# Who adds lam for the third row block, and where feed-forward's normalization reads and runs

## The chip, the cores and the metric

The kernel runs on one core of a Trainium2 chip. A core has a matrix engine (PE, with its weight loads shown as PEld), a vector engine (DVE), a scalar engine for activation functions (ACT), a general engine (POOL, called gpsimd in the code) and a queue engine that issues transfers (SP). Each runs its own queue of instructions in order; they meet through semaphores. Matmuls write to PSUM banks; DVE and ACT read both PSUM and SBUF, and POOL's instructions in this kernel read SBUF alone. The metric is the device time of one execution in microseconds (us).

## The reference

The input is `x` of 8 sequences, 512 tokens, 128 channels, all fp32. Two parts follow each other, each added to its input.

The first part normalizes `x` over channels, projects to 16 heads of 8 channels, and weighs causally, not with a softmax but with weights `1/(lam - s)`, where `lam`, one number for each query, is found by four Newton rounds:

```
lam = s_masked.max(-1) + 1.0
for _ in range(4):
    d = maximum(lam - s, EPS);  w = where(mask, 1/d, 0)
    f = w.sum(-1) - 1.0;        fp = -where(mask, 1/d**2, 0).sum(-1)
    lam = lam - f / fp
p = where(mask, 1/maximum(lam - s, EPS), 0);  p = p / p.sum(-1);  out = p @ V
```

The second part normalizes again and runs six layers. A layer is windowed attention (16 heads of 64 channels, windows of 32 keys with the window before, queries and keys normalized and rotated) and then feed-forward: shift half of the channels by one token, normalize over channels, scale and add, two matmuls to 341 columns each, gelu of one times the other, a matmul back to 128 columns.

## The kernel before

**Two parts woven together.** The first part of sequences 0 and 1 runs alone at the start, as two streams step by step. From about 600 us on the second part runs, sequence by sequence and layer by layer, and the first part of the other six sequences is fed in between. A unit is one layer of one sequence (48 of them); a unit takes eight slots, one for each pair of heads. A slot is one turn of the `while` loop, and `tick(n)` at twelve places in it lets the first part go on by a planned number of steps, so that the first part is used up at slot 232 of 384. After that the second part runs alone. Units go in groups: layers 0 to 5 of sequences 0 and 1 in turn (units 0 to 11), then sequences 2, 3 and 4, then 5, 6 and 7.

**A Newton round.** Four heads of a sequence make a batch; a batch has four rounds, and there are 32 batches, so 128 rounds. The scores lie negated in `ns`, one tile for each row block `rb` of 128 queries, in four pieces `a` of different width: a query sees only the keys up to its own 32-query piece, so block 3 has pieces of 416, 448, 480 and 512 columns, block 2 of 288, 320, 352 and 384, block 1 of 160 to 256, block 0 of 32 to 128. `lam` differs from piece to piece. A round needs `Ln(ns + lam)`, then `Exp(-that)`, which is the weight, then sums of the weights and of their squares, which DVE takes with one statistics instruction for each piece (L289). Seven short DVE instructions (`step`, L336 to L345) turn these into the new `lam`.

For blocks 3 and 2, `evaluations` lets ACT add `lam` itself, as the bias of the Ln; since the bias differs for each piece, that is one Ln for each piece (L301, four for a block). The Exp needs no bias and takes two pieces at once, a half of a block (L309). For blocks 1 and 0, `add_lam` (L276) has POOL add `lam` piece by piece into a tile `df`, and ACT takes the whole block with one Ln (L316) and one Exp (L321). In `newton`, POOL's adds are issued ahead of the ACT work of the round. After the fourth round of a batch the same `add_lam` adds the final `lam` to all four blocks (into `ns`, 16 instructions), and `attend_weigh` (L349, L351) takes Ln and Exp of these; this is issued in the first round of the next batch.

**Feed-forward.** `feed_forward` is a generator whose parts, between its `yield`s, are issued one by one by `further()`. While units of sequences 0 and 1 are under way (`dense`), there are four such places in each slot, otherwise one. The parts are: shift (POOL, L635 to L637); transpose into a PSUM bank `px` (PE, L833), copy it to SBUF as `xt` (ACT, L835), statistics from `xt` (DVE, L839 and L840); reciprocal deviation `rn` by Ln and Exp (ACT, L843 and L844) and the normalization of `xt` in four instructions (POOL, L846); transpose back (PE, L853) and scale and add (ACT, L855); the gate matmuls; gelu and the other matmuls; the last matmul and the sum.

**What sets the order.** The code's order gives priorities. The tile framework has a planner that fixes each engine's queue ahead of the run, by its own estimate of when an instruction's inputs are there, so a later instruction can stand ahead of an earlier one; `follow` is used where an order must hold. On the chip the queues then run in that order. PSUM banks for all of this come from one pool of five (`ps_a`, through `bank`). The tile `d` of a Newton round has two buffers of block 3's width; `df1` and `df0` have one each.

Of the kernel before, what the change touches and what calls it, by code (L numbers as in the profile page):

```python
# [9 lines left out]
F32 = mybir.dt.float32  # L10
BF16 = mybir.dt.bfloat16
AF = mybir.ActivationFunctionType
# [4 lines left out]
P = 128  # L17
# [33 lines left out]
def tile_kernel(  # L51
# [18 lines left out]
    nc = tc.nc  # L70
# [96 lines left out]
    def streams(pools, bank1):  # L167
# [70 lines left out]
        def width(rb):  # L238
            return sum(keys(rb, a) for a in range(4))
# [53 lines left out]
        def evaluations(t):  # L293

            late = []
            for rb in (3, 2):
                d = dp.tile([P, width(3)], F32, name="d")[:, 0 : width(rb)]
                for h in range(2):
                    for a in (2 * h, 2 * h + 1):
                        c = 4 * rb + a  # L300
                        nc.scalar.activation(  # L301
                            pieces(d, rb)[a], pieces(t["ns"][rb], rb)[a], AF.Ln,
                            bias=t["lam"][:, c : c + 1],
                        )
                    if late:
                        statistics(t, *late.pop(0))
                    yield
                    e = halves(d, rb)[h]
                    nc.scalar.activation(e, e, AF.Exp, scale=-1.0)  # L309
                    if late:  # L310
                        statistics(t, *late.pop(0))
                    yield
                    late += [(d, rb, 2 * h), (d, rb, 2 * h + 1)]
            for rb in (1, 0):
                d = t["df"][rb]
                nc.scalar.activation(d, d, AF.Ln)  # L316
                if late:
                    statistics(t, *late.pop(0))
                if rb:
                    yield  # L320
                nc.scalar.activation(d, d, AF.Exp, scale=-1.0)  # L321
                if late:
                    statistics(t, *late.pop(0))
                yield
                late += [(d, rb, a) for a in range(4)]
            for n in (3, 3, 2):
                for _ in range(n):
                    if late:
                        statistics(t, *late.pop(0))
                yield  # L330
# [87 lines left out]
        def stieltjes(seqs):  # L418
# [36 lines left out]
            def newton(now, k):  # L455
                if k == 0:
                    first_lam(now)
                    yield
                now["st"] = sm.tile([P, H, 2, 3], F32, name="stw")
                now["df"] = {}  # L460
                for rb in (1, 0):
                    now["df"][rb] = d = dp.tile([P, width(rb)], F32, name=f"df{rb}", bufs=1)
                    add_lam(now, d, rb)
                yield
                yield from evaluations(now)
                step(now)
                yield
# [359 lines left out]
    def feed_forward(u, w1, w2):  # L827
# [3 lines left out]
        px = bank([P, NT, D], "px")  # L831
        for c in range(NT):
            nc.tensor.transpose(px[:, c, :], xs[:, c * P : (c + 1) * P], ident)  # L833
        xt = tp.tile([P, NT, D], F32, name="xt", tag="ff")
        nc.scalar.copy(xt, px)  # L835
        st = tp.tile([P, NT, 6], F32, name="st")
        mv = tp.tile([P, NT, 2], F32, name="mv")
        for c in range(NT):
            nc.vector.bn_stats(st[:, c, :], xt[:, c, :])  # L839
            nc.vector.bn_aggr(mv[:, c, :], st[:, c, :])  # L840
        yield
        rn = tp.tile([P, NT], F32, name="rn")
        nc.scalar.activation(rn, mv[:, :, 1], AF.Ln, bias=eps_ln)  # L843
        nc.scalar.activation(rn, rn, AF.Exp, scale=-0.5)  # L844
        for c in range(NT):
            nc.gpsimd.tensor_scalar(  # L846
                xt[:, c, :], xt[:, c, :], mv[:, c, 0:1], rn[:, c : c + 1],
                ALU.subtract, ALU.mult,
            )
        yield  # L850
# [241 lines left out]
```

## Time and profile before

| | us |
|---|---|
| median of three runs | 4686.6 (4683.49 to 4689.29) |
| profiled execution | 4683.56 |
| its span, first to last instruction | 4681.8 |
| busy: PE, DVE, ACT, POOL | 4029.8, 3935.3, 3532.1, 3177.3 |
| L301, Ln with lam as bias, 1024 instructions | 590.4 |
| L309, Exp of blocks 3 and 2, 512 | 441.2 |
| L276, POOL's adds in the rounds, 1024 | 400.3 |
| L846, POOL's normalization in feed-forward, 192 | 150.2 |

How to read the lines below. A group line names the line of code, the engine, the operation, out<-in, shapes and the count, then the busy time and the mean of one instruction in ns, then the idle time of the engine just before it and what ended it. A line of waits says who waited for whom: us in total, times, the longest. The chain of waits is followed back from the last instruction, at each step to what released it; a piece shows its start, its length and who did it. A table by stretches of the span gives for each stretch its length, then each engine's busy time (and number of instructions), the granted clock, the share of the transfer engines and GB/s. `x4` at the end of a line means four instructions. Instructions that follow at once on ACT and DVE overlap by about a tenth of a microsecond, so that what one costs in a busy stretch is read from start to start.

### The profile page before, as it was taken

How to read it: one execution, taken by the hardware profiler on the slowest of the kernel's cores; microseconds unless marked ns; L12 is line 12 of the kernel's file. 1: busy time of each engine (PE TensorE's matmuls, PEld its weight loads, DVE VectorE, ACT ScalarE, POOL GpSimd, SP SyncE). 2: the span in 40 equal slices, each digit the busy share in tenths (PEclk: the TensorE clock that was granted, in tenths of full speed). 3: DMA queues.
4: the chain of work that ended last, by engine and by line, in shares of the span. 5: the costliest groups of instructions: out<-in, count | busy, mean ns of one | idle time of the engine just before them, and what ended most of it. 6: DMA issues, size and time to landing. Idle time of an engine off the chain costs nothing.

```text
span 4681.8 us, 165984 instructions
## 1 busy us (share of the span) xinstructions
PE 4029.8 (86%) x68749; PEld 2507.4 (54%) x68749; DVE 3935.3 (84%) x8788; ACT 3532.1 (75%) x6716; POOL 3177.3 (68%) x4081
## 2 busy tenths in 40 slices
PE   4344688887888888898988999998999999999998
PEld 1233455554455544555555555555666666666665
DVE  7878788887888888998998999999787788877785
ACT  7998677777788777888887888888666666666664
POOL 4543666666666666776777767777787777777774
PEclk7667799999999999999999999999999999999999
DMA  1000222222122222232222222222243333333332
GB/s 49 1 1 1 67 59 51 62 55 59 46 66 61 60 53 62 62 72 50 59 67 54 69 54 70 53 59 68 66 102 83 85 90 75 88 79 86 89 75 59
DMA packets 558912, 288.87 MB, mean 62 GB/s; under 512 B 97580, under 2 KB 541264, under 8 KB 558160
## 3 DMA queue, kind: packets, MB, share of 16 engines
q1 hardware_dynamic: 558160, 278.26, 25.4%
q8 instruction: 543, 8.90, 0.8%
q14 instruction: 209, 1.71, 0.1%
HBM read 66.21 MB, written 7.34 MB: 16 GB/s over the span
## 4 chain that ended last, share of the span: by engine, by line
PE 41%; ACT 26%; DVE 22%; POOL 8%; issue 2%; DMA 1%; SPq 1%; ACTq 0%; POOLq 0%; DVEq 0%
PE m L667 8%; ACT d L301 7%; ACT d L309 5%; PE ptq L733 4%; PE pv L704 4%; DVE stw L289 4%; PE acc L812 4%; DVE qr L672 4%; PE po L787 3%; PE s L752 3%; PE pT L776 3%; POOL ns L276 3%; DVE raw L689 3%; ACT sq L678 2%; PE s L263 2%
## 5 line engine op out<-in xcount | busy, mean ns | idle before, releaser
L682 POOL TENSOR_TENSOR qn<-qr 128x512 f32<-128x512 f32 x768 | 970.0, 1280 | 493.6 <-DVE qr L672 440.5
L672 DVE TENSOR_TENSOR qr<-m,tab 128x1024 f32<-128x1024 f32 x768 | 913.5, 1217 | 157.7 <-PE m L667 116.2
L695 POOL TENSOR_TENSOR qn<-qn,ss 128x512 f32<-128x512 f32 x768 | 786.3, 1046 | 299.5 <-ACT ss L692 285.2
L667 PE MATMUL m<-wqkv,xs 128*128 128x512 f32 x1536 | 759.4, 608 | 16.1 <-ACT prT L777 3.7
L678 ACT ACTIVATE sq<-m 128x512 f32<-128x512 f32 x768 | 459.5, 600 | 394.1 <-DVE qr L672 385.1
L301 ACT ACTIVATE d<-ns,lam 128x416 f32<-128x416 f32 (+7 forms) x1024 | 590.4, 625 | 91.6 <-DVE lam L345 71.0
L289 DVE BATCH_NORM_STATS2 stw<-d 128x6 f32<-128x480 f32 (+7 forms) x1024 | 545.8, 563 | 122.7 <-ACT d L309 120.3
L276 POOL TENSOR_TENSOR df<-ns,lam 128x160 f32<-128x160 f32 (+7 forms) x1024 | 400.3, 429 | 307.2 <-DVE sw L343 135.6
L763 POOL TENSOR_TENSOR pr<-pr,nm 128x512 f32<-128x512 f32 x384 | 401.2, 1045 | 253.2 <-DVE ss L690 146.2
L738 ACT COPY qT<-ptq 128x512 f32<-128x512 f32 x768 | 425.0, 586 | 184.5 <-PE ptq L733 183.4
L689 DVE TENSOR_REDUCE raw<-sq 128x16 f32<-128x1024 f32 x384 | 466.6, 1215 | 64.5 <-ACT sq L678 53.2
L733 PEld LDWEIGHTS ptq<-ident,qn 128*128 128x128 f32 x3072 | 364.7, 144 | 207.9 <-issue 110.4
L733 PE MATMUL ptq<-ident,qn 128*128 128x128 f32 x3072 | 428.2, 281 | 34.3 <-POOL qn L695 20.3
L812 PE MATMUL acc<-oT,wo 128*128 128x512 f32 x768 | 414.6, 622 | 39.0 <-ACT oT L808 38.1
L704 PE MATMUL pv<-wqkv,xs 128*128 128x256 f32 x1536 | 440.3, 410 | 7.7 <-ACT sq L678 5.8
L309 ACT ACTIVATE d<-d 128x864 f32<-128x864 f32 (+3 forms) x512 | 441.2, 871 | 0.0
L364 PE MATMUL dTp<-ident,ns 128*128 128x128 f32 x1280 | 231.3, 302 | 184.1 <-POOL ns L276 119.1
L667 PEld LDWEIGHTS m<-wqkv,xs 128*128 128x128 f32 x1536 | 259.8, 194 | 206.6 <-issue 136.6
L787 PE MATMUL po<-v,prT 64*32 64x65 f32 x24576 | 348.5, 226 | 20.3 <-DVE pr L757 19.7
L752 PE MATMUL s<-qT,qT 64*32 64x64 f32 x24576 | 355.8, 226 | 6.0 <-ACT qT L738 5.0
L787 PEld LDWEIGHTS po<-v,prT 64*32 64x32 f32 x24576 | 278.5, 106 | 129.8 <-issue 52.8
L263 PE MATMUL s<-kn,qj 32*32 32x288 f32 (+14 forms) x4096 | 321.2, 419 | 23.0 <-DVE mn L267 17.6
(137 smaller groups left out, 7984.3 us busy)
## 6 DMA issues: line engine op xcount, KB each, us to landing
v<-v SPq DMA_DIRECT2D x2304, 65.0 KB
v<-v SPq DMA_DIRECT2D x768, 48.8 KB
wqkv<-in_L_ffn_Wqkv_dram SPq DMA_DIRECT2D x72, 256.0 KB
v<-v SPq DMA_DIRECT2D x384, 32.5 KB
wqkv<-in_L_ffn_Wqkv_dram SPq DMA_DIRECT2D x72, 128.0 KB
wo<-in_L_ffn_Wo_dram SPq DMA_DIRECT2D x36, 256.0 KB
tab<-tabs SPq DMA_DIRECT2D x36, 256.0 KB
w<-in_L_ffn_W_dram SPq DMA_DIRECT2D x18, 341.0 KB
```

The costliest lines, as they stand in the source:

```text
L289: nc.vector.bn_stats(t["st"][:, 4 * rb + a].rearrange("p u k -> p (u k)"), pieces(d, rb)[a])
L301: nc.scalar.activation(pieces(d, rb)[a], pieces(t["ns"][rb], rb)[a], AF.Ln, bias=t["lam"][:, c : c + 1],)
L309: nc.scalar.activation(e, e, AF.Exp, scale=-1.0)
L667: nc.tensor.matmul(m.rearrange("p t h e -> p t (h e)"), lhsT=xs[:, c * P : (c + 1) * P], rhs=wqkv[:, 0:2, q0 : q0 + HQ * DHL], start=True, ...
L672: nc.vector.tensor_tensor(qr, m.unsqueeze(1).to_broadcast([P, 2, 2, HQ, DHL]), tab[:, i].rearrange("p (k t) e -> p k t e", k=2).unsqueeze( ...
L682: nc.gpsimd.tensor_tensor(g["qn"][:, c].rearrange("p t h (u e) -> p (t h) u e", u=2), halves_of[:, 0], halves_of[:, 1, :, ::-1, :], ALU.add,)
L689: nc.vector.tensor_reduce(raw[:, :, :, 0], sq, axis=AX.X, op=ALU.add)
L695: nc.gpsimd.tensor_tensor(qc, qc, ss[:, i, :].unsqueeze(2).to_broadcast([P, 2 * HQ, DHL]), ALU.mult)
L704: nc.tensor.matmul(pv[:, i], lhsT=xs[:, c * P : (c + 1) * P], rhs=cols, start=True, stop=True,)
L733: nc.tensor.transpose(pt[:, c * P : (c + 1) * P], g["qn"][:, c, t, 2 * p : 2 * p + 2, :].rearrange("p h e -> p (h e)"), ident,)
L787: nc.tensor.matmul(po[u * QB : (u + 1) * QB, e, c, :], lhsT=prT[rows, c, u * QB : (u + 1) * QB], rhs=g["v3"][rows, n, p, :], start=True, s ...
L812: nc.tensor.matmul(acc, lhsT=wo[:, pp % (NPAIR // 2), :], rhs=a["oT"], start=(pp == 0), stop=(pp == NPAIR - 1),)
```

## The change

In `evaluations`, block 2 goes the way of blocks 1 and 0: POOL adds `lam` to its four pieces, into a tile `df2` (first of the three blocks in `newton`), and ACT takes Ln of a half at a time, without bias, in place in `df2`. Block 3 stays as it was; its tile `d3` has one buffer, so that both blocks together need less room than the two buffers of `d` did.

In `feed_forward`, as long as the first part is not used up (`near`), the copy to `xt` is gone: the statistics read the transposed block in its PSUM bank, and DVE, not POOL, normalizes from the bank into `xt`. One `yield` is gone too, so that transpose, statistics, `rn` and normalization are issued as one part. After the first part has ended, feed-forward is as before.

```diff
@@ evaluations
             for rb in (3, 2):
-                d = dp.tile([P, width(3)], F32, name="d")[:, 0 : width(rb)]
+                d = dp.tile([P, width(3)], F32, name="d3", bufs=1) if rb == 3 else t["df"][2]
                 for h in range(2):
-                    for a in (2 * h, 2 * h + 1):
-                        c = 4 * rb + a
-                        nc.scalar.activation(
-                            pieces(d, rb)[a], pieces(t["ns"][rb], rb)[a], AF.Ln,
-                            bias=t["lam"][:, c : c + 1],
-                        )
+                    e = halves(d, rb)[h]
+                    if rb == 3:
+                        for a in (2 * h, 2 * h + 1):
+                            c = 4 * rb + a
+                            nc.scalar.activation(
+                                pieces(d, rb)[a], pieces(t["ns"][rb], rb)[a], AF.Ln,
+                                bias=t["lam"][:, c : c + 1],
+                            )
+                    else:
+                        nc.scalar.activation(e, e, AF.Ln)
...
@@ newton
-                for rb in (1, 0):
+                for rb in (2, 1, 0):
                     now["df"][rb] = d = dp.tile([P, width(rb)], F32, name=f"df{rb}", bufs=1)
                     add_lam(now, d, rb)
@@ feed_forward
+        near = done_steps < total
         xt = tp.tile([P, NT, D], F32, name="xt", tag="ff")
-        nc.scalar.copy(xt, px)
+        if not near:
+            nc.scalar.copy(xt, px)
+        src = px if near else xt
         st = tp.tile([P, NT, 6], F32, name="st")
         mv = tp.tile([P, NT, 2], F32, name="mv")
         for c in range(NT):
-            nc.vector.bn_stats(st[:, c, :], xt[:, c, :])
+            nc.vector.bn_stats(st[:, c, :], src[:, c, :])
             nc.vector.bn_aggr(mv[:, c, :], st[:, c, :])
-        yield
+        if not near:
+            yield
         rn = tp.tile([P, NT], F32, name="rn")
...
         for c in range(NT):
-            nc.gpsimd.tensor_scalar(
-                xt[:, c, :], xt[:, c, :], mv[:, c, 0:1], rn[:, c : c + 1],
+            (nc.vector if near else nc.gpsimd).tensor_scalar(
+                xt[:, c, :], src[:, c, :], mv[:, c, 0:1], rn[:, c : c + 1],
                 ALU.subtract, ALU.mult,
             )
```

More of the change, by code (lines that the diff above doesn't have):

```diff
@@ L307, in evaluations @@
                     yield
-                    e = halves(d, rb)[h]
                     nc.scalar.activation(e, e, AF.Exp, scale=-1.0)
```

## The prediction

> **What bounds the kernel now.** I read the busy table by stretches first, cut where the work changes: two streams of the first part (110 to 520 us), the woven stretch with units 0 to 10 (600 to 1880), the woven rest (1880 to 3260), the second part alone.
>
> ```profile
> core 0: us, PE busy (x) PEld busy (x) DVE busy (x) ACT busy (x) POOL busy (x), PEclk, DMA share, GB/s
> 110.00:520.00 410.00, 186.00 (x1837) 116.05 (x1837) 323.43 (x1101) 368.82 (x607) 191.72 (x409) 0.66 0.04 12
> 600.00:1880.00 1280.00, 1078.60 (x17486) 646.57 (x17486) 1088.95 (x2571) 998.52 (x1875) 837.28 (x1121) 0.94 0.24 57
> 1880.00:3260.00 1380.00, 1258.67 (x21566) 759.97 (x21559) 1259.78 (x2881) 1136.18 (x2172) 996.94 (x1291) 0.98 0.27 62
> 3260.00:4682.00 1422.00, 1393.94 (x26288) 925.54 (x26287) 1105.76 (x1740) 892.65 (x1817) 1043.42 (x1054) 0.99 0.35 81
> ```
>
> ACT is 90% busy in the first stretch; in the woven ones nobody is full (PE and DVE 84 to 91%, ACT 78 and 82%, POOL 65 and 72%); the last is PE's, and the change leaves it alone. So I next added up the chain of waits in each stretch: 110 to 520 is ACT 58%, DVE 22%, POOL 8%; 600 to 1880 is ACT 30%, DVE 27%, PE 25%, POOL 13%; 1880 to 3260 is ACT 36%, DVE 34%, PE 18%, POOL 8%. Before 110 ACT has 34%. These shares are my price of a microsecond: one on ACT after 1880 is worth 0.36.
>
> Pieces of that chain in the first stretch, two streams in step, give the costs of block 2:
>
> ```profile
> 204.54 1.76 ACT d L301 x4
> 206.30 1.20 ACT d L309 x2
> 207.50 1.97 ACT d L301 x4
> 209.46 1.41 ACT d L309 x2
> ```
>
> The reader is to see that two Lns with bias (288 and 320 columns) take 0.88 for a stream, the one Exp over the same 608 columns 0.60; for 352 and 384 it is 0.985 against 0.705.
>
> In the woven stretch with units 0 to 10, feed-forward stops everybody. Counting slots by their two copies L738, the two slots with feed-forward's middle take 19.3 us each, the others about 11.6. The chain there, then the timeline of the same place, then the waits of the stretch:
>
> ```profile
> 1000.80 3.12 POOL xt L846 x4
> 1003.92 0.04 issue
> 1003.97 0.48 PE pn L853
> 1004.44 1.71 PE ptq L733 x8
> ```
>
> ```profile
> 1004.48 0.78 ACT L855 ACTIVATE xn_ffn<-pn,vec 128x512 f32<-128x512 f32 x1 [4.28 <-PE pn L853]
> 1008.17 2.36 DVE L672 TENSOR_TENSOR qr<-m,tab 128x1024 f32<-128x1024 f32 x2 [8.37 <-PE m L667]
> ```
>
> ```profile
> PE pn L853 <- POOL xt L846: 53.3, 44, 9.7
> ACT xn_ffn L855 <- PE pn L853: 44.0, 11, 9.0
> ```
>
> PE stands before the transposes until POOL has normalized, ACT and DVE stand behind PE. All 44 normalizations of these 11 units are on the chain, 34.3 us.
>
> **Part 1, block 2 on ACT.** A round loses two Lns' starts and the bias reads: 0.88 + 0.985 - 0.60 - 0.705 = 0.56 us, in 128 rounds 72 us of ACT. By chain shares: 7 rounds before 110 (x 0.56 x 0.34 = 1.3), 30 to 520 (x 0.58 = 9.7), 43 to 1880 (x 0.30 = 7.2), 45 after (x 0.36 = 9.1). Gain 11.0 alone, 16.3 woven; 72 at the very most, nothing at least, if `lam` still comes from DVE when it does now.
>
> **Part 1, block 2 on POOL.** The same adds exist after each batch:
>
> ```profile
> L276 POOL TENSOR_TENSOR ns<-ns,lam 128x384 f32<-128x384 f32 x32 | 26.6, 831 | 0.0
> L276 POOL TENSOR_TENSOR ns<-ns,lam 128x352 f32<-128x352 f32 x32 | 24.9, 777 | 0.0
> L276 POOL TENSOR_TENSOR ns<-ns,lam 128x320 f32<-128x320 f32 x32 | 23.1, 723 | 0.0
> L276 POOL TENSOR_TENSOR ns<-ns,lam 128x288 f32<-128x288 f32 x32 | 21.4, 669 | 0.1
> ```
>
> A round pays 3.00 us, ahead of the 3.4 of blocks 1 and 0; 128 make 384 us, POOL's share rises from 0.65 to 0.73 and from 0.72 to 0.79 in the woven stretches (feed-forward's normalization taken off).
>
> Is ACT kept waiting? It takes block 3 first. From the start of POOL's first add to ACT's first Ln of block 2 there are 5.7 us (median) in the first woven stretch, 4.7 in the second, and the two pieces it wants take 1.39. Put in front of the present adds, they would be late three times in 128, 7 us together: I take nothing for it. The cover is block 3's four Lns and two Exps.
>
> What is queued behind on POOL pays: `qn` (L682, L695; PE's transposes and the two `qr` buffers wait for these), `pr` (L763; ACT's Exp), the adds for `attend_weigh`. I pushed POOL's queue back by 3 us after each round's adds, less the idle time met on the way, and compared each end with its consumer's start. Feed-forward's own part left out, some consumer would be late in 6 of 43 rounds of the first woven stretch and in 11 of 45 after; the worst lateness of each such round sums to 21 and 44 us. That is the ceiling, 65, if each moves the end. By chain share it is 3.0 x 43 x 0.105 (POOL's 13% without L846) = 13.5 and 3.0 x 45 x 0.08 = 10.8: 24. A queue that meets idle time forgives, so I take 24, floor zero.
>
> Alone, POOL has room (47% busy) except in the first round of a batch, where the 6 us of both streams go ahead of 19 us of `attend_weigh` adds: compared likewise, ACT would wait 1.7, 1.7, 3.0 and 6.0 more, 12 in all; the planner can put other ACT work first, and I take 4.
>
> DVE pays too. Its short instructions with two operands in SBUF last longer when POOL is at work:
>
> ```profile
> L338 DVE TENSOR_TENSOR stw<-s,stw x128: 156/204/1283, 48.6 to 3269.9; 128x32 f32<-128x32 f32 x128
> L345 DVE SCALAR_TENSOR_TENSOR lam<-sw,lam x128: 150/174/972, 55.8 to 3273.9; 128x16 f32<-128x16 f32 x128
> ```
>
> (minimum, median and maximum ns.) L336, L338, L342, L344 and L345 together lie 0.83 us a round over what they take beside an idle POOL. A tenth more POOL is 0.083 x 88 rounds x 0.3 = 2. The Trainium skill's page SBUF — State Buffer, section SBUF: two separate sides, speaks against the change here: DVE and GpSimd share a port pair that whoever starts first holds for a whole instruction, and a DVE instruction with two SBUF inputs is blocked until then. By that rule each of the five would wait half of a 0.75 us add with 0.07 more probability, which is 0.13 x 88 = 12 us of DVE, an estimate, twice the trace's 7 before shares. The trace's own maxima (1283 against 156) agree with blocking; the sum keeps 2.
>
> `d3` with one buffer costs nothing: the next round's first Ln needs `lam`, and `lam` needs all statistics of this one.
>
> **Part 2, feed-forward, units 0 to 10.** POOL's four at 798 ns go (34.3), DVE's four come. No row shows a per-partition normalization from PSUM of 128 columns; L382, a 128-column copy from PSUM, has 278 ns, L864, scalar addition from PSUM, 740 at 512 columns, which less 384 columns at the 1.04 ns of L289's rows is 339. I take 330, nearest the operation: 14.5 us. Gain 20. POOL also began 19 us later, summed over the 11, than `rn` was done, because it was at `qn`, `pr` or adds; DVE is idle just there (8.37 above), but has its own queue, so half: 9.5. The copy frees 0.60 x 11 of ACT, x 0.30 = 2. Statistics from the bank cost what they did (278 from PSUM against 269). Together 31.5. Floor 10: with the `yield` gone DVE stands at the normalization until ACT has done `rn` (0.52 us plus up to 1.6 of ACT's queue), and behind it stand `qr` and the statistics, on which POOL and ACT wait. Ceiling 60: all 44 us that ACT stands before L855, and what follows being issued a quarter of a slot earlier. The bank `px` is held until the normalization instead of until the copy, some 4 us, one of five; PE is stopped in that time anyway, so nothing.
>
> **Part 2, units 11 to 27.** Here feed-forward waits for nobody (L846 hardly shows in the chain), so there is little to win: DVE +17 x 1.32 x 0.34 = 7.5 lost; DVE standing for `rn`, 1 us each, 6 lost; ACT 17 x 0.60 x 0.36 = 3.7 and POOL 17 x 3.13 x 0.08 = 4.3 won. Net 5.5 lost, between 8 won and 25 lost. No transfer is issued elsewhere, and SP's queue is passed by nothing.
>
> **Sum.** -11 + 4 (alone), -16.3 + 24 + 2 (woven rounds), -31.5 + 5.5 (feed-forward) = -23 us on the profiled 4683.6, which is 3.0 under the median: 4686.6 - 23 = 4664 after rounding, 0.5% faster.
>
> **Rivals.** *POOL's added adds decide (slower).* Place: `qn` and `pr` behind the adds. For it: POOL has 13% of the chain at only 65% busy, and 17 rounds with late consumers. Against it: the other 71 rounds meet idle time soon enough. Without its term the sum is -47, so it decides from 47 of the 65 on; at the ceiling the time is 4686.6 - 47 + 65 = 4705. *The stop at feed-forward only changes its owner.* DVE's queue takes POOL's place and the gain is the floor, 10: about 4686, no change. For it: DVE is 85% busy there. Against: its 8 us of idle at that very place. *The stop goes altogether*, for which speak ACT's 44 us: 60 in place of 31.5, time 4635.
>
> **How the numbers follow.** A measurement of this kernel tells about 0.2% (9 us) from no change. Forecast 0.44, stop gone 0.14, owner changed 0.15, POOL decides 0.27. The forecast alone spans 4640 to 4680 and its upper edge is in the band of no change. Faster 0.57, same 0.14, slower 0.29. The range reaches from "stop gone" with POOL's adds at their floor (4635 - 24 = 4611) to POOL at its ceiling with feed-forward at its floor (4705 + 21.5 = 4726).
>
> **What would show it.** L301 has 512 instructions, L276 in the rounds 1536, POOL's busy time grows by about 384 - 28 x 3.13 = 300, ACT's falls by 72 + 17 = 89, DVE's grows by 37 or more. Right: in the two feed-forward slots of units 0 to 10 PE's wait before L853 falls under 20 us in sum and the slots to about 17.7; up to 520 us the same work ends about 7 us sooner. Wrong: waits of PE, ACT or DVE for L682, L695 and L763 that grow by more than 50 us; ACT before block 2's Ln waiting for POOL; or a new wait of DVE for `rn`. The planner orders all queues anew, which can move the woven stretches either way by an amount no row of before tells.

## The result: 0.4% slower, and the profile after

The changed kernel takes 4706.13 us (median of five executions, 4702.6 to 4708.96) against 4687.67 (4683.49 to 4689.73) for the kernel before, beside which it was run: 18.5 us more, ratio 1.0042 [1.0031, 1.0054]. The forecast was 4664, faster. The profiled execution took 4707.44 us, its span is 4705.7, which is 23.9 over the span before; places are compared below between profiled executions, so that their sums are held against 23.9, not 18.5.

The table by stretches of the kernel after, with the columns of before (length, busy time of PE, PE's weight loads, DVE, ACT and POOL with the number of instructions, granted clock, share of the transfer engines, GB/s):

```profile
core 0: us, PE busy (x) PEld busy (x) DVE busy (x) ACT busy (x) POOL busy (x), PEclk, DMA share, GB/s
110.00:520.00 410.00, 194.35 (x1817) 117.73 (x1818) 325.06 (x1091) 347.19 (x532) 268.70 (x525) 0.62 0.04 11
600.00:1880.00 1280.00, 1085.30 (x17778) 649.38 (x17777) 1121.74 (x2660) 978.20 (x1797) 934.29 (x1267) 0.94 0.25 58
1880.00:3260.00 1380.00, 1244.64 (x21008) 747.71 (x21006) 1247.52 (x2863) 1086.07 (x2024) 1053.87 (x1382) 0.98 0.26 61
3260.00:4700.00 1440.00, 1411.81 (x26718) 937.88 (x26716) 1128.53 (x1796) 908.69 (x1851) 1055.43 (x1070) 0.99 0.35 81
```

What was meant to move has moved. In the first stretch ACT is 22 us less busy and POOL 77 more, in the woven ones ACT 20 and 50 less, POOL 97 and 57 more; 1880 to 3260 also holds less of everybody's work, since the same work now takes longer. The groups of the adds and of the Ln with bias, after:

```profile
L276 POOL TENSOR_TENSOR df<-ns,lam 128x288 f32<-128x288 f32 (+11 forms) x1536 | 761.3, 533 | 218.8 <-DVE lam L348 97.8
L303 ACT ACTIVATE d<-ns,lam 128x416 f32<-128x416 f32 (+3 forms) x512 | 324.2, 677 | 116.4 <-DVE lam L348 101.4
```

The counts are those announced, 1536 and 512 (lines lie two or three further down in the code after, up to seven in feed-forward). ACT's idle time just before these Lns was 91.6 us in the kernel before (L301) and is 116.4 now: ACT has less to do and waits longer for `lam`.

Block 2's Ln costs what was said. Pieces of the chain of waits, after (start, length, who):

```profile
284.91 0.60 ACT df L308
285.51 0.36 ACT ns L354
285.87 0.60 ACT df L308
```

Two pieces (608 columns) take ACT 0.60 us, where two Lns with bias took 0.88.

The stop at feed-forward has gone from units 0 to 10. The waits of 600 to 1880, after:

```profile
PE pn L860 <- DVE xt L853: 8.0, 6, 3.0
ACT xn_ffn L862 <- PE pn L860: 2.2, 2, 2.0
```

These were 53.3 and 44.0. Who holds the chain in the first stretch has changed as well. The shares by line between 110 and 520 us, the first line from before, the second from after:

```profile
by line: ACT d L301 21.2%; ACT d L309 15.5%; DVE stw L289 10.6%; ACT ns L351 5.1%; ACT df L316 5.1%; DVE dT L367 4.9%; ACT ns L349 4.9%; ACT df L321 4.3%; PE po L378 3.7%; POOL ns L276 3.4%; issue 2.8%; PE s L263 2.6%; POOL df L276 2.0%; DV
```

```profile
by line: DVE stw L289 15.7%; POOL df L276 13.7%; POOL ns L276 10.8%; DVE dT L370 8.2%; PE s L263 6.0%; issue 5.3%; PE po L381 4.5%; ACT d L303 3.2%; DVE s L339 3.1%; ACT d L312 3.0%; ACT df L308 2.6%; ACT df L312 2.4%; ACT df L319 2.2%; ACT
```

ACT's 58% have become 17, POOL's 8% have become 27 and DVE's 22% have become 37. ACT was relieved so far that other engines took its place.

**Where the time went.** A slot can be found in every trace by ACT's two copies `qT`. The start of the same slot in two profiled executions, one minus the other, gives the lead or loss up to there. The marks are slot 8 (617 us in before), slot 96 (1831), slot 224 (3309, shortly before the first part is used up). Feed-forward of units 0 to 10 lies between the first two, that of units 11 to 27 nearly all between the last two. The last column ends at the last slot. In us against before:

```
                       to slot 8   8 to 96   96 to 224   after 224
after                     +8.8      -20.5      +35.9       +0.9
forecast                  -7        -24         +8          0
```

(The forecast's parts, put to their stretches: -7.2 + 13.5 + 1 - 31.5 and -9.1 + 10.8 + 1 + 5.5.) The stretch with the stop came out nearly as forecast, but by luck, as the last part shows. The loss is at the start, 16 us off the forecast, and in units 11 to 27, 28 off.

How well such a reading repeats: four kernels below (e2, e3, e5, e6) have the same code in units 0 to 10 and read -22.7, -24.6, -24.9 and -21.7 in the second column. Kernels below that leave units 11 to 27 as they were (e7, e10, e11, and e3 but for unit 11) read +2 to +8 in the third; what is left there is the planner's new order and the state in which they enter. Seven whose code at the start is that of before (e2, e3, e5, e6, e10, e11, e17) read +0.2 to -3.6 in the first. So about 4 us in the first column, 3 in the second and 8 in the third mean nothing. The columns come from one profiled execution of each kernel: their sums differ by up to 7 us from the difference of the medians, and in e10, whose profiled execution is its fastest, by 9.

### The profile page after: what moved, and what is told of

It is laid out like the page before. It is cut to its first block, busy times and chain, and to the rows that moved or that the text cites. A ratio compares the mean times of both kernels' runs of the same rounds, so it can differ in the third digit from the quotient of the medians.

```text
span 4705.7 us, 166329 instructions
## 1 busy us (share of the span) xinstructions
PE 4048.6 (86%) x68749; PEld 2510.4 (53%) x68749; DVE 3984.4 (85%) x8900; ACT 3449.2 (73%) x6430; POOL 3447.3 (73%) x4481
## 4 chain that ended last, share of the span: by engine, by line
PE 40%; ACT 23%; DVE 22%; POOL 10%; issue 3%; DMA 1%; SPq 0%; ACTq 0%; POOLq 0%; DVEq 0%
PE m L670 7%; DVE stw L289 5%; PE pv L707 4%; PE ptq L736 4%; PE acc L815 4%; ACT d L303 4%; PE po L790 3%; POOL ns L276 3%; DVE qr L675 3%; POOL df L276 3%; PE s L755 3%; DVE raw L692 3%; ACT d L312 3%; PE pT L779 2%; ACT sq L681 2%
## 5 line engine op out<-in xcount | busy, mean ns | idle before, releaser
L276 POOL TENSOR_TENSOR df<-ns,lam 128x288 f32<-128x288 f32 (+11 forms) x1536 | 761.3, 533 | 218.8 <-DVE lam L348 97.8
L289 DVE BATCH_NORM_STATS2 stw<-df 128x6 f32<-128x160 f32 (+11 forms) x1536 | 482.5, 360 | 46.4 <-ACT df L324 24.1
L736 PE MATMUL ptq<-ident,qn 128*128 128x128 f32 x3072 | 418.6, 277 | 44.4 <-POOL qn L698 22.9
L303 ACT ACTIVATE d<-ns,lam 128x416 f32<-128x416 f32 (+3 forms) x512 | 324.2, 677 | 116.4 <-DVE lam L348 101.4
L790 PE MATMUL po<-v,prT 64*32 64x65 f32 x24576 | 359.0, 228 | 28.7 <-DVE pr L760 28.3
L289 DVE BATCH_NORM_STATS2 stw<-d 128x6 f32<-128x416 f32 (+3 forms) x512 | 306.6, 630 | 58.2 <-ACT d L312 57.9
```

The costliest lines, as they stand in the source:

```text
L276: nc.gpsimd.tensor_tensor(o, n, by.to_broadcast([P, keys(rb, a)]), ALU.add)
L289: nc.vector.bn_stats(t["st"][:, 4 * rb + a].rearrange("p u k -> p (u k)"), pieces(d, rb)[a])
L736: nc.tensor.transpose(pt[:, c * P : (c + 1) * P], g["qn"][:, c, t, 2 * p : 2 * p + 2, :].rearrange("p h e -> p (h e)"), ident,)
L790: nc.tensor.matmul(po[u * QB : (u + 1) * QB, e, c, :], lhsT=prT[rows, c, u * QB : (u + 1) * QB], rhs=g["v3"][rows, n, p, :], start=True, s ...
```

## Experiments: the two halves of the change alone

Is the loss POOL's added adds, or feed-forward?

e1_block2: the changes to `evaluations` and `newton`, with `feed_forward` as before. Its core:

```diff
-                for rb in (1, 0):
+                for rb in (2, 1, 0):
...
+                    else:
+                        nc.scalar.activation(e, e, AF.Ln)
```

> The first part of the change alone: POOL adds lam for block 2, feed-forward as before. The changed kernel came out 18.5 us slower; by equal slots it lost 9 us before the second part is under way, won 20 in units 0 to 10, lost 36 in units 11 to 27. Theory POOL (the added adds cost it, in the rest above all): about 9 us lost before slot 8, 5 to 15 in units 0 to 10, 25 to 35 in units 11 to 27, near 4730 in all. Theory FEED (DVE's normalization and its stop for rn cost it in units 11 to 27): only the 9 us at the start are lost and the woven stretches win up to 8, near 4690. Theory ORDER (the planner's new order, not any one cost): the effects of this run and the next do not add up to the changed kernel's, by more than 15 us.

e2_ffn: the changes to `feed_forward` alone. Its core:

```diff
+        near = done_steps < total
...
-        yield
+        if not near:
+            yield
...
-            nc.gpsimd.tensor_scalar(
+            (nc.vector if near else nc.gpsimd).tensor_scalar(
```

> The second part alone: feed-forward from its bank while the first part lasts, block 2 on ACT as before. Theory POOL: the start is unchanged, 25 to 35 us are won in units 0 to 10, units 11 to 27 lose no more than 8, near 4660. Theory FEED: about 25 us are won in units 0 to 10, 25 to 35 lost in units 11 to 27, near 4690. Theory ORDER: neither sum holds.

Measured: e1 4750.49 against 4685.91, ratio 1.0141 [1.0125, 1.0156], 64.6 us slower. e2 4691.6, ratio 1.0014 [1.0005, 1.0023], 5.7 slower. By stretches:

```
              to slot 8   8 to 96   96 to 224
e1_block2        +7.2      +26.0      +32.5
e2_ffn           -3.6      -22.7      +30.8
after            +8.8      -20.5      +35.9
```

Neither half is any good alone, and they don't add: 70 apart, 18.5 together. So e1 by itself went roughly as POOL said (with more lost in units 0 to 10), e2 by itself as FEED said, and the sum of the two misses by 52 us, which is ORDER's sign; that the planner's order is the reason is not shown by it. Feed-forward gives 23 of the 31.5 forecast in units 0 to 10 and loses all of it in the rest, where a loss of 5.5 was forecast. Block 2 alone costs 26 and 32, near the ceiling of the rival *POOL's added adds decide* (21 and 44); together with feed-forward's part it costs 2 and 5.

## Experiments: what feed-forward's three edits do

The diff in `feed_forward` holds three things that the prediction had in one sum: statistics from the bank without the copy, normalization on DVE, and one `yield` less. Two theories for the gain in units 0 to 10: the shorter normalization does it (call it NORM), or that what follows is issued a quarter of a slot earlier (EARLIER).

e3_ffn_early, e2 only while units 0 to 11 are under way, and e10 and e11, which part the edits there:

```diff
 # e3: e2, but
-        near = done_steps < total
+        near = len(groups_of) > 1 and b in groups_of[0]
 # e10: before, without the yield in units 0 to 10
-        yield
+        if u > 10:
+            yield
 # e11: bank and DVE in units 0 to 10, the yield kept
+        near = u <= 10
...
-        if not near:
-            yield
+        yield
```

> The second part alone and only for sequences 0 and 1 (units 0 to 11), block 2 on ACT as before. Both theories: 25 to 35 us won in units 0 to 10 and nothing moved before or after, 4653 to 4662. By POOL it differs from the run with all 28 units by less than 8 us, by FEED it is 25 to 35 us faster than that.

> Units 0 to 10 lose only the yield; copy on ACT and normalization on POOL stay, block 2 and the other units as before. All of feed-forward's change there won 24 us from slot 8 to 96. Theory NORM (POOL's 3.1 us and its queue were the stop): 0 to 8 of the 24. Theory EARLIER (issuing the rest a quarter of a slot sooner did it): 14 to 24.

> Units 0 to 10: statistics from the bank and normalization on DVE, but the yield kept between them; everything else as before. Theory NORM: 16 to 24 of the 24 us from slot 8 to 96. Theory EARLIER: 0 to 8.

Measured: e3 4665.77 against 4685.91, 0.9960 [0.9948, 0.9973]; e10 4703.23 against 4682.51, 1.0044 [1.0029, 1.0059]; e11 4640.02, 0.9912 [0.9897, 0.9927]. In units 0 to 10 (slots 8 to 96): e3 -24.6, e10 +8.5, e11 -46.7. Two kernels below with the same code there as e11 read -45.6 (e14) and -50.0 (e17). The whole of e3 came out 26 us under e2, as FEED said.

NORM is right, EARLIER falls: the missing `yield` costs 8.5 alone (by e10's median the loss is larger, 21 us in the whole) and 22 on top of the shorter normalization. Waits of 600 to 1880 in e10, then in e11:

```profile
PE pn L854 <- POOL xt L847: 51.1, 44, 9.5
ACT xn_ffn L856 <- PE pn L854: 44.8, 11, 9.5
```

```profile
ACT xn_ffn L858 <- PE pn L856: 14.4, 9, 6.3
PE pn L856 <- DVE xt L849: 13.0, 9, 3.4
```

The reader is to see that the wait is no measure of the time here: e11 waits 14.4 us before `xn_ffn`, e3 and after only 2.3 and 2.2, and e11 is the faster by 22. What the milestones of a unit say (means in us after the first transpose into `px`, over units 0 to 10):

```
                     normalized   gate matmuls start   gelu starts   last matmul ends
before                  12.3            19.4              26.4            31.8
e10 (yield gone)        12.1            14.3              26.8            32.3
e11 (bank, DVE)          8.7            14.9              22.7            28.4
e3 (both)                7.9            10.9              22.7            28.1
```

Without the `yield` the gate matmuls start 4 to 5 us sooner, and gelu comes no sooner at all. So PE's time for the gate is taken from other work ahead of need; that this is where the 22 us go was not tried apart. The mean length of a slot by its place among eight: the two slots with feed-forward's middle last 20.0 and 19.8 us before, 16.9 and 19.4 in e11, 20.9 and 16.5 in e3; the other six together 70.6, 69.8 and 70.7. Both orders shorten one slot by three; without the `yield` the long slot is 1.5 longer than in e11, the short one 0.4 shorter and the six 0.8 longer.

One thing is not parted from this, the granted clock of PE. Between slots 8 and 96 its mean was 0.937 in before, 0.930 in e10, 0.947 in e3 and 0.961 in e11, in the order of the times, and PE's busy time for the same work was 1021.9, 1020.7, 1010.2 and 1004.9 us. In before the clock was halved 24 times in this stretch, each time behind 3.4 us in which PE had been busy for 55% or less. So a shorter stop of PE can bring the higher clock; no run holds the clock fixed, and how much of the 47 and the 22 came by it is open.

**The rest, units 11 to 27.** e5 does e2 there but keeps each later part in its old slot; e6 does e2's edits only in units 0 to 10 and takes away only the `yield` in the rest; e17 is e2 with the `yield` kept throughout; e13 shifts everything after the normalization one slot later (and has e7's start, below).

```diff
 # e5: e2, and after the normalization, for the units after the tenth
+        if near and u > 10:
+            yield
 # e6
+        near = u <= 10
+        early = done_steps < total
-        if not near:
+        if not (near or early):
             yield
 # e17: e2, but
-        if not near:
-            yield
+        yield
 # e13: before pn, units after the tenth, while the first part lasts
+        if not near and done_steps < total:
+            yield
```

> Feed-forward from its bank as long as the first part lasts, block 2 on ACT as before; but for units 11 to 27 one empty part is put behind the normalization, so that the gate matmuls, gelu and all that follows stay in the slots that they had before. Feed-forward alone lost 31 us from slot 96 to 224, with slot 6 of the eight grown from 11.0 to 13.8 us. Theory SLOT (the missing yield moves the gate, gelu and its table loads into slots where they cost more): the loss falls to 8 or less, 4655 to 4668 in all. Theory DVE (the four instructions and the stop for rn on DVE cost it): the loss stays at 22 to 31, 4680 to 4692.

> The other way round: feed-forward from its bank for units 0 to 10 alone; units 11 to 27 keep the copy on ACT and the normalization on POOL and lose only the yield. Theory SLOT: 20 to 30 us lost from slot 96 to 224, near 4688. Theory DVE: at most 8 lost there, 4655 to 4668.

> Feed-forward from its bank on DVE in units 0 to 27 with the yield kept in its old place, block 2 on ACT as before. Units 11 to 27 hold the bank for a whole slot then. If the missing yield was what units 11 to 27 lost by, and not the bank or DVE: 0 to 8 lost from slot 96 to 224, 4640 to 4648. If DVE's 1.6 us and the bank held longer cost too: 10 to 25 lost, 4650 to 4665.

> The fastest so far (feed-forward from its bank for units 0 to 10, block 2 on POOL in later rounds while the first part is alone, 4657), with one empty part more in feed-forward of units 11 to 27, so that the gate, gelu and what follows come one slot later, not earlier. If what counts is which of the two alternating kinds of slot gets gelu, it loses 20 to 35 as one slot earlier did: 4678 to 4692. If the earlier slots are worse because they lie before the unit's boundary, later is no worse or better: 4640 to 4660.

Measured: e5 4682.94 against 4686.19, 0.9990 [0.9982, 0.9999]; e6 4693.22, 1.0017 [1.0008, 1.0026]; e17 4660.1 against 4686.53, 0.9942 [0.9927, 0.9957]; e13 4667.64 against 4682.51, 0.9969 [0.9958, 0.9980]. From slot 96 to 224:

```
e3   as before                                 +7.6
e5   bank and DVE, old slots                   +18
e17  bank and DVE, yield kept                  +26
e6   yield gone only                           +35
e2   all three                                 +31
e13  as before, one slot later                 +11.6  (and +8 after slot 224)
```

Taking away the `yield` costs 27 (e6 less e3), normalizing on DVE from the bank 10 to 19 (e5 and e17 less e3), and both together 23, less than their sum. So SLOT and DVE both hold in part, and e17 came out as the second of its two cases. e13's time lies between its two ranges: one slot later costs 7 here against e7 (+4.2), no more than such a reading can tell. In this stretch one `yield` is a whole slot: gelu starts 46.0 us after the first transpose in before, 47.1 in e17, 37.5 in e2 and e6. What it meets there can be read from the chain of waits: how much of it between 1880 and 3300 us is gelu on ACT with the two loads of its tables (L822, L824 in before; each load 1.28 us, gelu 1.48). e16, described further down, has the adds on POOL and the normalization as before, and is to be held against e1:

```
yield kept     before 19.0   e1 16.4   e3 16.2   e5 19.0   e7 19.0   e17 16.4   e13 32.4
yield gone     after 47.3    e2 36.5   e6 39.2   e16 23.0
```

Without the `yield`, in after, e2 and e6, gelu's 4 us on ACT lie where others wait for ACT: 17 to 31 us more of the chain than in before, in e6 23 more than in e3, against a loss of 27. But this share does not follow the loss everywhere: in e16 it is only 7 more than in e1, with 21 lost, and in e13 13 more than in e7, with 7 lost. Who waits shows in the waits of 1880 to 3260, in before and then in e6:

```profile
ACT qT L738 <- PE ptq L733: 42.5, 34, 2.4
PE acc L812 <- ACT oT L808: 12.1, 18, 1.2
PE ptq L733 <- DVE gate L875: 6.0, 4, 2.0
```

```profile
ACT qT L738 <- PE ptq L733: 49.5, 29, 4.5
PE acc L812 <- ACT oT L808: 23.3, 28, 2.1
PE ptq L733 <- DVE gate L880: 16.8, 11, 2.1
```

PE waits 11 us more for ACT's `oT` and 11 more for DVE's gate, the product with gelu's result, before it can transpose the queries. This second wait is the sign that goes with the `yield`: 12.4 to 16.8 us in all four kernels without it (after, e2, e6, e16), 5.6 to 6.9 in all the others. That gelu's move to another place costs the 27 is thus argued from chain and waits; no run moved gelu alone. For the 10 to 19 of the DVE normalization no single wait carries it. The forecast had 7.5 + 6 for it, and the difference lies within what the third column can't tell.

## Experiments: block 2 at the start

e9_relief takes the work from ACT without giving it to POOL: block 2's Ln goes over two pieces at once with the first piece's `lam` as bias for both, and the scores are scaled by 1e-6. This leaves out the second piece's own `lam` and the size of block 2's scores, so that its weights mean nothing; all else is done in full. ACT's gain is 0.37 us a round (the bias read stays) in place of 0.56.

```diff
+                    else:
+                        c = 4 * rb + 2 * h
                         nc.scalar.activation(
-                            pieces(d, rb)[a], pieces(t["ns"][rb], rb)[a], AF.Ln,
-                            bias=t["lam"][:, c : c + 1],
+                            halves(d, rb)[h], halves(t["ns"][rb], rb)[h], AF.Ln,
+                            bias=t["lam"][:, c : c + 1], scale=1e-6,
```

> The gain on ACT without POOL's adds: block 2 takes one Ln for each half, with the lam of the half's first piece as the bias of both pieces and the scores scaled by 1e-6 so that it stays positive (the second piece's own lam and the scores' share are left out of the computation, feed-forward as before). This takes 0.56 - 2 x 0.09 = 0.37 us a round from ACT. Chain shares price it at 7 us before slot 0, 5 in units 0 to 10, 6 after: 4668. Rival (the woven stretches are not moved by ACT): the 7 at the start at most, 4679 to 4686. With POOL's adds alone 65 us slower, the adds themselves would then cost 65 plus this gain.

e12_adds_no_relief does the reverse: e1's adds on POOL, but ACT still takes block 2 with four biased Lns (over the added tile, which it overwrites, so that the adds are for nothing).

```diff
-                    if rb == 3:
+                    if rb > 1:
```

> POOL's adds for block 2 without the gain on ACT: POOL adds into df2, and ACT then takes the four Lns with bias from the scores all the same and overwrites the sums (it waits for POOL as in the run with block 2 on POOL alone; the adds' results are not used). Feed-forward as before. Against that run, which lost 7 to slot 8, 26 to 96 and 32 to 224: if ACT's time is worth nothing in the woven stretches, the loss there is the same within 5 each, and only the start is 10 to 20 later; near 4763. If ACT's time is worth its chain share there (7 and 9), the loss grows by that: near 4780.

e7_alone_later_rounds has feed-forward's part in units 0 to 10, and block 2 on POOL only while the first part runs alone, and not in the first round of a batch, where the adds for `attend_weigh` lie.

```diff
 # e7: block 2 in newton, and in evaluations
+                now["two"] = k > 0 and done_steps < 5 * STEPS
...
-                    add_lam(now, d, rb)
+                    if rb < 2 or now["two"]:
+                        add_lam(now, d, rb)
...
-                    if rb == 3:
+                    if rb == 3 or not t["two"]:
```

> Feed-forward from its bank for units 0 to 10; POOL adds lam for block 2 only while the first part runs alone, and there only in the second to fourth round of a batch; elsewhere ACT does as before. Theory BURST (what cost 7 to 9 us at the start is the first round of a batch, where POOL has 31 us of adds in a round of 28): the start is 5 to 9 us faster than the kernel before at slot 8, and the whole 4655 to 4661. Rival (POOL's adds cost in every round, or DVE is next and takes the gain): the start stays within 2 us of before or is later, 4664 to 4672.

Measured: e9 4671.73 against 4686.19, 0.9968 [0.9955, 0.9980]; e12 4745.39 against 4682.51, 1.0135 [1.0120, 1.0151]; e7 4657.34 against 4686.19, 0.9937 [0.9925, 0.9950]. By stretches:

```
                          to slot 8   8 to 96   96 to 224
e9_relief                   -15.4      -2.4       +4.3
e12_adds_no_relief          +15.2     +21.8      +22.8
e1_block2 (both)             +7.2     +26.0      +32.5
e7_alone_later_rounds       -11.8     -19.0       +4.2
```

Two things follow. First, a microsecond taken from ACT is worth all of itself at the start (40 rounds up to slot 8, x 0.37 = 14.8; measured 15.4) and nothing that shows in the woven stretches, though ACT has 30 and 36% of the chain there: e9 gains 2.4 and loses 4.3, where the chain shares gave gains of 5 and 6, and e1 with ACT's relief is no faster than e12 without it. By its total, 4671.73, e9 comes near the 4668 of the chain shares, but its whole gain lies at the start. Second, at the start the adds hurt in particular rounds. By the ends of the rounds, after is 2.2 us ahead after the first batch's four and 2.9 after the second's. Then two rounds lose 10.2 and 7.6: the first rounds of the third and the fourth batch, 31 us long for 21 before in the one case, 33 for 24 in the other. The chain of waits in the first of these two, after:

```profile
220.90 2.79 POOL df L276 x8
223.69 0.27 issue
223.96 2.87 POOL ns L276 x3
226.83 5.88 POOL df L276 x12
232.71 7.11 POOL ns L276 x9
```

From 218 to 240 us the chain is POOL adding `lam`, 12.8 us for the rounds of both streams (2 x (3.0 + 3.4)) and 19 for the final `lam`, together as long as the round. e7, which leaves the first rounds alone, ends 11.8 ahead in place of 8.8 behind (some 5.5 of its lead are lost in each of the two first rounds all the same and won back in the rounds behind them; from what, no run shows), and between 110 and 520 us its chain is ACT's again, with 54%. So BURST holds, with more won than the 5 to 9 expected:

```profile
by line: ACT d L303 10.9%; DVE stw L289 10.8%; ACT d L312 8.9%; ACT df L312 6.7%; ACT ns L354 5.6%; ACT ns L352 5.1%; ACT df L319 4.7%; ACT df L308 4.6%; ACT df L324 4.5%; DVE dT L370 4.0%; POOL ns L276 3.4%; issue 2.8%; ACT df L303 2.7%; P
```

## Experiments: why the adds cost 26 and 32 alone, and 2 and 5 in the change

Two theories: POOL is free of the normalization and so has room for the adds (call it LOAD), or the missing `yield` makes room (YIELD). e4 is after with feed-forward's part only in units 0 to 11. e15 frees POOL of the normalization in units 0 to 10 and keeps the `yield`. e16 is e1 without the `yield`, POOL keeping the normalization.

```diff
 # e4: after, but
-        near = done_steps < total
+        near = len(groups_of) > 1 and b in groups_of[0]
 # e15: after, but
-        near = done_steps < total
+        near = u <= 10
-        if not near:
-            yield
+        yield
 # e16: e1, and
-        yield
+        if done_steps >= total:
+            yield
```

> Both parts, but feed-forward's part only for units 0 to 11. Theory POOL: within 8 us of the changed kernel, 4698 to 4706. Theory FEED: units 11 to 27 lose nothing any more, 4670 to 4678.

> POOL adds lam for block 2 in every round, together with feed-forward from its bank with the yield kept, in units 0 to 10 alone. The two parts of the change cost 65 and 6 us one by one but 18.5 together. Theory LOAD (the adds cost only because POOL also had feed-forward's normalization): the adds lose 5 or less against the run with the bank and yield alone (which won 47 from slot 8 to 96), so 42 to 47 are won there, while units 11 to 27, where POOL still normalizes, lose 24 to 32. Theory YIELD (the adds cost little only where the yield is gone, because the order is another): 20 to 30 of the 47 are lost in units 0 to 10 too.

> POOL adds lam for block 2 in every round, and units 0 to 27 lose only the yield; copy on ACT and normalization on POOL stay. Theory LOAD: the costs of the adds (26 from slot 8 to 96, 32 to 224) and of the missing yield (8.5 and 27 to 35) add up: 34 and 60 to 67, near 4785. Theory YIELD: with the yield gone the adds cost 2 to 5, so 10 to 14 and 32 to 40 are lost, near 4740.

Measured: e4 4698.49 against 4685.91, 1.0026 [1.0015, 1.0037]; e15 4699.35 against 4686.53, 1.0027 [1.0017, 1.0036]; e16 4782.3, 1.0207 [1.0190, 1.0224]. What the adds cost, each time one kernel less the one without the adds (for the last place e16 less e6, which differ in units 0 to 10 too):

```
feed-forward's part          units 0 to 10                 units 11 to 27
as before                    e1  26                        e1 32.5, e4 less e3 17, e15 less e11 21
bank and DVE, yield kept     e15 less e11  23              -
yield gone only              e16 less e10  30              e16 less e6  19
all three                    after less e2  2, e4 less e3 4   after less e2  5
```

Neither theory holds alone: with POOL freed and the `yield` kept the adds cost 23 (as YIELD said of e15), with the `yield` gone and POOL not freed 30 and 19 (e16's total lies near LOAD's 4785). They are cheap only where all three edits are made. e4 lies in POOL's range, 4698 to 4706. What the adds do to POOL's queue is the same each time: from the end of `qr` on DVE to the end of `qn` there are 2.75 us before, 3.63 in e1 and 3.50 in after, in units 0 to 10, and 2.80, 3.51 and 3.42 in the rest. So a `qn` comes 0.6 to 0.9 us later in both, and costs time in the one and hardly any in the other. That the missing `yield` and the adds spend the same slack, so that whichever comes second is nearly free, fits where feed-forward normalizes on DVE: there the missing `yield` costs 22 without the adds and 3 with them (after and e4, each less e15). It does not fit e16, where POOL normalizes and the two costs add up. Why the adds are cheap in the change stays open.

## Experiment: what beats both kernels

e14 puts together what was found good: e11's feed-forward (bank and DVE in units 0 to 10, the `yield` kept) and e7's adds (alone, not in first rounds).

```diff
 # e14: e7, but
-        if not near:
-            yield
+        yield
```

> What the runs so far point to, in one kernel: in units 0 to 10 statistics from the bank and normalization on DVE with the yield kept (47 us won there); units 11 to 27 as before; POOL adds lam for block 2 only while the first part runs alone, in the second to fourth round of a batch (8 to 12 us won at the start). If the two are independent: 4630 to 4635.

Measured: 4640.06 against 4686.53, 0.9901 [0.9886, 0.9916], 46.5 us faster than before. e11 alone had 0.9912 [0.9897, 0.9927]; the two can't be told apart by these intervals, and e14 is 5 us above the 4635 expected. By stretches e14 leads by 9.4 at the start (e11: 3.1), gains 45.6 in units 0 to 10 and loses 5.7 in the rest.

## Why the prediction was wrong, step by step

Two terms turned the sign: units 11 to 27 of feed-forward, +5.5 in the forecast and +31 when made alone (e2), and block 2 at the start, -11 + 4 in the forecast and +8.8 in the result. Term by term:

- **The price by chain share (-11 and -16.3).** 0.56 us a round on ACT was right (ACT's busy time fell by 83, forecast 72 + 17 = 89). "One on ACT after 1880 is worth 0.36" is the step that failed. At the start a microsecond was worth one, not 0.34 to 0.58, as long as POOL stayed off the chain (e9); in the woven stretches no gain showed (e9). The chain goes through ACT there; that the other engines are close behind, their busy shares of 65 to 91% make likely, but no run shows it.
- **POOL's adds, woven (24, ceiling 65).** As part of the whole change they cost 2 and 5, below the forecast; alone 26 and 32, near the rival's ceiling. The prediction treated this term as independent of feed-forward's, and the runs show it isn't.
- **POOL's adds, alone (4, ceiling 12).** Mis-sized: the place was right (first rounds of a batch, 6 us ahead of 19), but two rounds lost 17.8 between them. "The planner can put other ACT work first" failed: a round that is all POOL has nothing to put first. -11 + 4 came out as +8.8.
- **DVE's short instructions (2).** Small, as forecast. Between slots 8 and 224 the five lasted 5 us less in after than before. The estimate of 12 by the Trainium skill's rule on the port pair (SBUF — State Buffer, section SBUF: two separate sides) is not borne out by these sums: they are 14 more in e1, but 3 and 4 more in e12 and e16 with the same adds, and 11 more in e13, which has no such adds in these rounds.
- **ACT before block 2's Ln waiting for POOL (0).** Right in size: 9.1 us in five waits over the whole span, half of it in the woven stretches:

```profile
its engine sat idle before it (us, times) until:
  POOL df L276: 9.1, 5
```

- **Feed-forward, units 0 to 10 (-31.5).** The sum was 9 to 11 too high (-20.5 in after, -22.7 in e2), and its make-up was not right. That the whole stretch came to -20.5 for -24 was luck: this gain was 9 smaller, the gain on ACT (7) did not show, and POOL's adds cost 11 less than forecast. The edits to the normalization alone gave 46.7, above the forecast and near the rival *The stop goes altogether*; "what follows being issued a quarter of a slot earlier" was put down as a gain in that rival's ceiling, and cost 22. PE's wait before the transposes fell under 20 as announced, the two slots only to 18.6 in the median (19.3 before), not 17.7. The new instruction, after:

```profile
L853 DVE TENSOR_SCALAR xt<-px,mv,rn 128x128 f32<-128x128 f32 x112 | 38.0, 401 | 4.7 <-ACT rn L851 4.2 <-POOL df L276 0.2
```

  One lasts 0.40 us, but four overlap, 38.0 for 112 or 0.34 each, against 0.33 forecast (of the two rows it was taken from, 740 ns less 384 columns at 1.04 ns is 341, not 339, which changes nothing). DVE stood 4.2 us for `rn` in 28 units: the rival *The stop at feed-forward only changes its owner* had little in it. Statistics from the bank cost what was said, 274 ns for 270.
- **Feed-forward, units 11 to 27 (+5.5, from -8 to +25).** This is the term with the largest error, +31 in e2. It was made of busy times by chain shares, and what it left out was the move: there one `yield` is a whole slot, taking it away costs 27 by itself (e6 less e3) and 21 on top of the adds (e16 less e1), and PE's wait for the gate behind gelu doubles (6.0 us in before, 15.2 in after). That ACT's block of gelu and its table loads is what costs is argued, as said above. The normalization on DVE adds 10 to 19 of its own. "No transfer is issued elsewhere" weighed the transfers that the move could touch, and not ACT's and DVE's work.
- **The caveat on the planner** was sound but small: kernels with the same code in a stretch differ by up to 3 us in units 0 to 10 and by 2 to 8 from before in the rest.

- **The signs to look for.** None of those named for a wrong forecast came: no wait for L682, L695 or L763 grew by 50 us (ACT's for L763 grew most, from 1.7 to 15.0), and DVE stood for `rn` only the 4.2 us said above. Between 600 and 3300 us the wait for POOL that grew most is ACT's before `attend_weigh`, from 34.5 to 62.5, a place that the prediction names but gives no sign for. The signs were all of one kind, a wait for POOL or for `rn`, and the loss lay in what the missing `yield` moved and in two rounds full of POOL.

The sum: 15.8 us wrong at the start, 3.5 in units 0 to 10, 27.9 in the rest, 0.9 behind it; -23 + 48.1 = 25.1 at the last slot, 23.9 at the end. The time is that of the rival *POOL's added adds decide* at its ceiling, 4705, but for other reasons: those adds cost 7 in the woven part and not 65.

## What to carry to other kernels

A share of the chain is no price of a microsecond where several engines take turns: there the relief of one showed no gain, while the start, where one engine had 58%, paid it in full until the next engine was full, so add up every engine's work round by round and not on the mean. When an edit takes out an issue boundary, price it apart from the work it saves: ask which long block moves to which place, and who waits there. Split such a change into its edits before judging it; here two of feed-forward's three edits, in 11 of 28 units, were worth 42 us (e11), and the change that contained them lost 18.

## What the hardware showed that was not expected

- A wait that vanishes need not be time gained: ACT's wait before `xn_ffn` fell from 44.0 to 14.4 us in e11 and to 2.3 in e3, and e3 is the slower by 22 us in the same units.
- The same delay of 0.6 to 0.9 us in POOL's `qn` went with a loss of 26 and 32 us in one kernel (e1) and of 2 and 5 in another (after less e2).
- A normalization with two per-partition scalars from PSUM took DVE 401 ns for 128 columns, and a copy from PSUM of as many 278.
